# The order of 16 small products in a convolution round: down the columns of TensorE's tiles, or along the diagonals

## The chip, the core and the metric

The kernel runs on one core of a Trainium2 chip. The metric is the device time of one execution in microseconds (us); lower is better. Three runs of the kernel before took 5010.55, 5017.47 and 5027.52 us; the median is 5017.47 us. A core has five engines, each with an instruction stream of its own: TensorE (PE in the profile; its weight loads are listed apart as PEld), VectorE (DVE), ScalarE (ACT), GpSimd (POOL) and SyncE (SP, which only issues transfers here).

## What is computed

Two layers on a tensor of 4 x 512 x 64 x 64 in fp32. The first is a linear attention with a multi-scale branch; the second works on image gradients. Cut to the part that bears on the change:

```
q, k, v = h @ wq.T, h @ wk.T, h @ wv.T                       # 512 channels each
dw = conv(qkv, dw_kernel, groups=3*512)                      # 5x5, one filter per channel
pw = conv(dw, pw_kernel, groups=3*64)                        # 1x1, 8 channels to 8
f = concat(qkv, pw).reshape(B, -1, 24, N)                    # heads of 8 + 8 + 8 channels
query, key = relu(f[:, :, :8]), relu(f[:, :, 8:16]); value = f[:, :, 16:]
out = (value_pad @ key.T) @ query, divided by its last row
y = bn(conv1x1(out, proj_kernel)) + x
# second layer: Sobel, Laplace and diagonal gradients of y, four 1x1 branches with
# GELU, channel attention, a 1x1 fuse, layer norm over channels, GELU, + y
```

The change is in the pair `dw`, `pw` for keys and queries: a 5x5 convolution per channel and then a mix of 8 channels to 8. The kernel does both at once, as one 5x5 convolution from 8 channels to 8 whose weights are the products of the two.

## The kernel before

For each of the 4 images, four groups of 128 channels are worked through (class `Group`). A group first makes keys and values (`keys_and_values`), then queries (`queries`). Projections (`project`, line 268) leave a 128 x 512 strip: 128 channels, and 8 rows of the image that lie 4 apart. Line 283 copies each strip by four transfers on ScalarE's queue into the input tile of the convolution, `inps[t]`, of shape [128, 4, 17, 64]: the partition is 32 i + 4 x (channel in its eight) + (row modulo 4), the second index n picks one of four blocks of channels, the third is a block of four image rows.

`convolve` (line 394) does one half of the image for keys or queries: 2 kinds x 2 halves x 16 groups = 64 calls. It takes four PSUM banks (`quad_tiles`), one for each row group i of 32 partitions. A call has ten rounds: five horizontal offsets dx, in the order 0, -2, -1, 1, 2, and two vertical blocks b. A round has 16 products of 32 x 32 weights with 32 x 512 data (504 or 496 columns where dx cuts off the border). Product (i, j) reads rows 32 i to 32 i + 31 of the input's block j, so it uses row group i of TensorE, and writes partitions 32 j to 32 j + 31 of bank i, so it uses column group j. TensorE's array of 128 x 128 thus works as 16 tiles of 32 x 32, and in a round each tile gets one product. All ten rounds add up in the same banks.

After the call, ScalarE takes each bank through a Relu (line 415 for keys, line 421 for queries), and later `conv_turn`, `correlate`, `conv_denominators` and `conv_divide` use what it leaves. The weights `mat` are made by GpSimd (line 247); there are two buffers for them, so the next ones wait until `convolve` has finished with the old.

The order of TensorE's instructions is written out by hand: the pool context of line 107 (`manual_schedule` for TensorE) keeps it as the program issues it. `keys_and_values` and `queries` list the steps of a group with an estimate of TensorE time each, and in `run` every step is followed by so much of the later stages of the image before (projection out, line 661; edge maps and branches, line 738; fuse, line 848) as falls due by those estimates. `convolve` is one step, of estimate 10.6. Nothing else is put between its 160 products. The waits between engines are semaphores that the framework attaches to the first instruction which needs them.

Of the kernel before, what the change touches and what calls it, by code (L numbers as in the profile page):

```python
# [83 lines left out]
def _span(d, n):  # L84

    return max(0, -d), n - max(0, d)
# [3 lines left out]
def conv_seq_kernel(  # L90
    ctx: ExitStack, tc, x, wqkv, dpk, wtab, proj, projc, pwk, bn0, consts, vec, watt1, batt1, watt2, wbr, wfuse, out
):
    nc = tc.nc
# [15 lines left out]
    def work_tile(name, n=512):  # L109
        return work.tile([P, 512], F32, tag="w", name=name)[:, :n]  # L110
# [4 lines left out]
    def quad_tiles(name):  # L115
        return [psum.tile([P, 512], F32, tag="quad", name=name) for _ in range(4)]

    def squares(ap):

        return ap.rearrange("p (b x n) -> p n x b", b=4, n=4)  # L120

    def rows(ap, width=W):
        return ap.rearrange("p (r c) -> p r c", c=width)
# [21 lines left out]
    inps = {}  # L145
# [80 lines left out]
    class Group:  # L226
# [167 lines left out]
        def convolve(self, t, half):  # L394
            banks = quad_tiles("cv")
            last = len(DXS) * 2 - 1
            for n, (dx, b) in enumerate((dx, b) for dx in DXS for b in range(2)):
                c0, c1 = _span(dx, W)
                for j in range(4):
                    for i in range(4):  # L400
                        q = slice(32 * i, 32 * i + 32)
                        nc.tensor.matmul(  # L402
                            rows(banks[i])[32 * j : 32 * j + 32, :, c0:c1],
                            lhsT=self.mat[t][q, j, (dx + 2) * 8 + 4 * b : (dx + 2) * 8 + 4 * b + 4, :],
                            rhs=inps[t][q, j, 8 * half + b : 8 * half + b + 8, c0 + dx : c1 + dx],
                            start=(n == 0), stop=(n == last),
                        )
            outs = []
            for i in range(4):
                o = work_tile("co")  # L410
                if t == KEY:
                    if half == 0 and i == 0:
                        self.ksum = mini.tile([P, 4, 4], F32, name="ksum")
                    for a in range(2):
                        nc.scalar.activation(  # L415
                            o.rearrange("p (n a x b) -> p a n x b", n=4, a=2, b=4)[:, a],
                            squares(banks[i][:, 256 * a : 256 * a + 256]), AF.Relu,
                            accum_out=self.ksum[:, 2 * half + a, i : i + 1],
                        )
                else:  # L420
                    nc.scalar.activation(o, banks[i], AF.Relu)
                outs.append(o)
            self.conv[t] = outs
# [536 lines left out]
    for n, cur in enumerate(groups):  # L960
# [5 lines left out]
        if n and n % NG == 0:  # L966
            last = groups[n - 1]
# [8 lines left out]
    last = groups[-1]  # L976
# [142 lines left out]
```

## Time and profile before

| What | us |
|---|---|
| median of three runs | 5017.47 |
| the profiled execution | 5033.35 |
| its span, from the first instruction to the last | 5031.6 |
| TensorE busy with matmuls in it | 4694.3 |
| of which line 402, the products of `convolve` | 728.3 |
| VectorE busy | 2083.3 |
| ScalarE busy | 1581.8 |

The granted clock of TensorE averages 0.971 in this execution. Times in the sums below are made against the profiled execution and then set against the median. In a row of the groups, "x" is the number of records, "busy" the time in which at least one of them ran, and "mean" the length of a single one. The records of matmuls overlap, and their ends are modelled, so the mean of a matmul (593 ns at line 402) is no price; the distance between starts is. A row's last part says how long the engine was idle before its instructions and what ended that. "issue" there means that nothing the profile shows was being waited for.

### The profile page before, as it was taken

To read this page: it belongs to the slowest core of one execution; us is meant where nothing else is said; L and a number is where in the kernel's file an instruction comes from. 1 tells how busy PE (TensorE), PEld (TensorE's weight loads), DVE (VectorE), ACT (ScalarE), POOL (GpSimd) and SP (SyncE) were. 2 spreads that over 40 slices of the span, in tenths; PEclk is the share of its full clock that TensorE was granted. 3 is DMA by queue.
4 is the path that set the end of the run, shared out by engine and by line. 5 is a ranking of instruction groups with operands and counts; after the bars stand their busy time and mean duration, and the time that the engine had idled before them with its cause. 6 is when DMAs were issued, how large, how long until landed. Compare 5 with 4: busy or idle time off the path is not lost. (4 is left out here: it accounts for less than half of the span.)

```text
span 5031.6 us, 106279 instructions
## 1 busy us (share of the span) xinstructions
PE 4694.3 (93%) x46140; PEld 2689.2 (53%) x46140; DVE 2083.3 (41%) x2761; ACT 1581.8 (31%) x2712; POOL 397.3 (8%) x298
## 2 busy tenths in 40 slices
PE   9999999999999999799899999989999899899887
PEld 5655654455666554354465656445446565444333
DVE  1222222115565533311355553441125555447955
ACT  2112111003454423200245442430014445214765
POOL 0000000000000012100000000220000000000445
PEclk9999999999999999899999999999999999899998
DMA  6434467775666566677565566647665555575435
GB/s 198 138 119 134 134 192 194 162 163 161 193 190 189 180 187 189 192 177 167 152 189 189 186 192 183 207 153 217 149 173 176 171 173 170 162 166 144 165 125 163
DMA packets 627940, 864.04 MB, mean 172 GB/s; under 512 B 324073, under 2 KB 381449, under 8 KB 609041
## 3 DMA queue, kind: packets, MB, share of 16 engines
q1 hardware_dynamic: 548880, 756.51, 52.4%
q10 hardware_dynamic: 78592, 100.74, 6.3%
q8 instruction: 362, 5.93, 0.5%
q14 instruction: 106, 0.86, 0.1%
HBM read 575.93 MB, written 213.98 MB: 157 GB/s over the span
## 5 line engine op out<-in xcount | busy, mean ns | idle before, releaser
L268 PE MATMUL proj<-xt,w_sb 128*128 128x512 f32 x2048 | 955.9, 610 | 56.7 <-DMA xt<-in_x 34.6
L661 PE MATMUL yps<-hd,fold_sb 128*128 128x512 f32 x2048 | 907.8, 599 | 18.5 <-DMA hd<-heads 16.2
L402 PE MATMUL cv<-inp,mat 32*32 32x512 f32 x20480 | 728.3, 593 | 36.0 <-issue 28.2
L268 PEld LDWEIGHTS proj<-xt,w_sb 128*128 128x128 f32 x2048 | 382.7, 194 | 528.0 <-issue 451.6
L661 PEld LDWEIGHTS yps<-hd,fold_sb 128*128 128x128 f32 x2048 | 386.1, 191 | 511.0 <-issue 458.8
L402 PEld LDWEIGHTS cv<-inp,mat 32*32 32x32 f32 x20480 | 419.8, 103 | 313.1 <-issue 151.9
L848 PE MATMUL zps<-ef,wf_sb 128*128 128x512 f32 (+1 forms) x1056 | 473.4, 601 | 36.4 <-DMA ef<-ef 19.4
L290 PEld LDWEIGHTS val<-w_sb,xt 128*128 128x128 f32 x4096 | 470.6, 192 | 33.2 <-issue 25.9
L290 PE MATMUL val<-w_sb,xt 128*128 128x128 f32 x4096 | 485.2, 277 | 0.1
L738 PE MATMUL br<-maps,wbr_sb 128*128 128x256 f32 (+1 forms) x1792 | 474.2, 418 | 3.7 <-DVE s_sb L335 2.9
L274 ACT COPY strip<-proj 128x512 f32<-128x512 f32 x256 | 149.3, 583 | 932.5 <-PE proj L268 912.0
L666 DVE SCALAR_TENSOR_TENSOR yt<-yps,shift,xr 128x512 f32<-128x512 f32 x128 | 96.0, 750 | 836.5 <-PE yps L661 780.0
L738 PEld LDWEIGHTS br<-maps,wbr_sb 128*128 128x128 f32 x1792 | 340.9, 193 | 146.9 <-issue 102.0
L457 PE MATMUL corr<-near,ckt 128*32 128x160 f32 x8192 | 333.7, 315 | 40.3 <-DMA near<-near 32.9
L848 PEld LDWEIGHTS zps<-ef,wf_sb 128*128 128x128 f32 x1056 | 205.3, 198 | 285.5 <-issue 235.9
L247 POOL TENSOR_TENSOR mat<-dp_sb 128x1280 f32<-128x1280 f32 x32 | 76.7, 2398 | 3484.8 <-PE cv L402 2882.9
L457 PEld LDWEIGHTS corr<-near,ckt 128*32 128x32 f32 x8192 | 257.2, 111 | 136.1 <-issue 78.6
L714 DVE TENSOR_TENSOR maps<-dv 128x1054 f32<-128x1054 f32 (+1 forms) x112 | 158.0, 1411 | 376.3 <-PE br L738 376.2
L318 ACT ACTIVATE kt<-tr 128x512 f32<-128x512 f32 x128 | 75.9, 593 | 529.8 <-PE tr L316 401.2
L366 DVE RECIPROCAL rec<-rec 128x512 f32<-128x512 f32 x64 | 214.4, 3351 | 1.7
L746 ACT ACTIVATE ef_o<-br,shift,scale 128x256 f32<-128x256 f32 (+1 forms) x224 | 131.4, 590 | 228.1 <-PE br L738 210.4
L415 ACT ACTIVATE co<-cv 128x256 f32<-128x256 f32 x256 | 94.0, 398 | 331.1 <-PE cv L402 310.6
(127 smaller groups left out, 4049.2 us busy)
## 6 DMA issues: line engine op xcount, KB each, us to landing
xt<-in_x SPq DMA_DIRECT2D x316, 512.0 KB
near<-near SPq DMA_DIRECT2D x512, 264.0 KB
inp<-strip ACTq DMA_DIRECT2D x1024, 64.0 KB
win<-y SPq DMA_DIRECT2D x96, 396.0 KB
near<-vt SPq DMA_DIRECT2D x512, 66.0 KB
y<-yt SPq DMA_DIRECT2D x128, 264.0 KB
heads<-q SPq DMA_DIRECT2D x128, 256.0 KB
cheads<-cq SPq DMA_DIRECT2D x128, 256.0 KB
```

What stands on the lines that cost most here:

```text
L268: nc.tensor.matmul(ps, lhsT=self.w[t][:, c, :], rhs=xs[self.b, j][c], start=(c == 0), stop=(c == NCH - 1))
L274: nc.scalar.copy(s, ps)
L290: nc.tensor.matmul(ps[:, ts(c, P)], lhsT=xs[self.b, j][n][:, ts(c, P)], rhs=self.w[VALUE][:, n, :], start=(n == 0), stop=(n == NCH - 1),)
L366: nc.vector.reciprocal(rec, rec)
L402: nc.tensor.matmul(rows(banks[i])[32 * j : 32 * j + 32, :, c0:c1], lhsT=self.mat[t][q, j, (dx + 2) * 8 + 4 * b : (dx + 2) * 8 + 4 * b + 4, :],
L457: nc.tensor.matmul(self.banks[jj][32 * i : 32 * i + 32, 160 * b : 160 * b + 160], lhsT=self.held["c", i][:, at : at + 32], rhs=v[:, 4 * n ...
L661: nc.tensor.matmul(ps, lhsT=fold_sb[g // NG][:, g % NG, ts(c, P)], rhs=hd[g], start=(g == 0), stop=(g == 2 * NG - 1),)
L666: nc.vector.scalar_tensor_tensor(yt[:, :, 1 : W + 1], rows(ps), shift0[:, c : c + 1], rows(xr), ALU.add, ALU.add)
L714: nc.vector.tensor_sub(flat[:, half : 3 * half - 2], dvs[:, 2 : 2 * half], dvs[:, 0 : 2 * half - 2])
L738: nc.tensor.matmul(rows(ps), lhsT=wbr_sb[:, k, c, :], rhs=rows(maps[:, slot[k], c % 2, :], WB)[:, :, 0:W], start=(c == 0), stop=(c == NCH ...
L746: nc.scalar.activation(o[:, n, :], parts[n], AF.Gelu, bias=shift1[:, k : k + 1], scale=scale1[:, k : k + 1], accum_out=pool_sb[:, k, u : u ...
L848: nc.tensor.matmul(ps, lhsT=wf_sb[:, k, ts(c, P)], rhs=ef[k], start=(k == 0), stop=(k == 3))
```

## The change

The two loops of a round, j outside and i inside, become one loop over the 16 pairs. It runs over d from 0 to 3 outside and i inside, and takes j = (i + d) modulo 4. Before, the order is (0,0), (1,0), (2,0), (3,0), (0,1), (1,1) and so on. After, it is (0,0), (1,1), (2,2), (3,3), (0,1), (1,2), (2,3), (3,0) and so on. The products themselves, their operands and the flags for the first and last round stay the same, and nothing else in the kernel is edited.

```diff
@@ -396,15 +396,15 @@
             last = len(DXS) * 2 - 1
             for n, (dx, b) in enumerate((dx, b) for dx in DXS for b in range(2)):
                 c0, c1 = _span(dx, W)
-                for j in range(4):
-                    for i in range(4):
-                        q = slice(32 * i, 32 * i + 32)
-                        nc.tensor.matmul(
-                            rows(banks[i])[32 * j : 32 * j + 32, :, c0:c1],
-                            lhsT=self.mat[t][q, j, (dx + 2) * 8 + 4 * b : (dx + 2) * 8 + 4 * b + 4, :],
-                            rhs=inps[t][q, j, 8 * half + b : 8 * half + b + 8, c0 + dx : c1 + dx],
-                            start=(n == 0), stop=(n == last),
-                        )
+
+                for i, j in ((i, (i + d) % 4) for d in range(4) for i in range(4)):
+                    q = slice(32 * i, 32 * i + 32)
+                    nc.tensor.matmul(
+                        rows(banks[i])[32 * j : 32 * j + 32, :, c0:c1],
+                        lhsT=self.mat[t][q, j, (dx + 2) * 8 + 4 * b : (dx + 2) * 8 + 4 * b + 4, :],
+                        rhs=inps[t][q, j, 8 * half + b : 8 * half + b + 8, c0 + dx : c1 + dx],
+                        start=(n == 0), stop=(n == last),
+                    )
```

## The prediction

> **What bounds the kernel now.** I read the page first, for the engine that is always busy and the share of the changed line in it.
>
> ```profile
> span 5031.6 us, 106279 instructions
> PE 4694.3 (93%) x46140; PEld 2689.2 (53%) x46140; DVE 2083.3 (41%) x2761; ACT 1581.8 (31%) x2712; POOL 397.3 (8%) x298
> ...
> L402 PE MATMUL cv<-inp,mat 32*32 32x512 f32 x20480 | 728.3, 593 | 36.0 <-issue 28.2
> ...
> L402 PEld LDWEIGHTS cv<-inp,mat 32*32 32x32 f32 x20480 | 419.8, 103 | 313.1 <-issue 151.9
> ```
>
> TensorE is busy 93% of the span and everything else far less, so a microsecond won or lost inside a convolution is a microsecond of the kernel, nearly one for one. The changed line has 728.3 + 36.0 us. Its 20480 records are two per product of the program (64 calls x 10 rounds x 16 products = 10240): an fp32 product appears as two passes, each with its own weight load.
>
> The question is then what holds a round. I took one call that waits for nobody, the one at 191.67 us, and read the weight loads in order of time, then the sums of that window (columns: PE, then PEld, then clock, DMA share, GB/s):
>
> ```profile
> 191.67 0.23 PEld L402 LDWEIGHTS cv<-inp,mat 32*32 32x32 f32 x32 [0.17 <-issue]
> 192.13 0.10 PEld L402 LDWEIGHTS cv<-inp,mat 32*32 32x32 f32 x1 [0.22 <-issue]
> 192.56 0.55 PEld L402 LDWEIGHTS cv<-inp,mat 32*32 32x32 f32 x32 [0.32 <-issue]
> 193.42 8.02 PEld L402 LDWEIGHTS cv<-inp,mat 32*32 32x32 f32 x255 [0.31 <-issue]
> ...
> 191.67:202.35 10.68, 10.64 (x320) 6.55 (x320) 1.00 0.39 100
> ```
>
> All 32 loads of the first round go out in 0.23 us, then nothing for 0.22 us, one load, and again nothing. So the call is not short of issue speed at its start; it fills something and then waits. It takes 10.68 us, and 1.07 us per round. The passes alone, if all 16 tiles streamed all the time, need less: pass after pass on one tile is 427 ns apart at 512 columns, 420 at 504 and 413 at 496 (starts of single records), which is 2 x (2 x 427 + 4 x 420 + 4 x 413) = 8.37 us for the ten rounds. About 2 us of each call is therefore not streaming, 64 x 2 = 128 us in the kernel. This is all that any order of the products could win.
>
> Where do the 2 us go? I followed single records in that call, in ns after its first load. A product's life is: load 26, first pass 420, 4 until the second pass, 420 of that pass, and then 191 more until something is released. The release is seen like this: the load of product k starts 611 ns after the start of the second pass of product k-17 (619 at 512 columns, 604 at 496, so always the pass plus 191), for every k I followed. Between those two lie 16 products x 4 records = 64 records. So the stream behaves as a window of fixed length: 17 products per 26 + 420 + 4 + 420 + 191 = 1061 ns, 62.4 ns per product, 998 ns per round. Ten rounds give 9.98 us, and with the last drain and the uneven start the 10.68 of the row.
>
> **The change part by part.** It removes and adds no instruction: the same 160 products per call, in another order inside each round of 16. Three things move.
>
> First, the rows. Before, i runs inside, so the row groups are 0,1,2,3,0,1,2,3; after, i runs inside again, the same sequence. Each product's predecessor on its own tile stays exactly 16 back, and bank i is still finished by product 12+i of the last round, so the Relu of line 415 or 421 that waits for a bank is released at the same place. The four waits for free banks stay at products 0 to 3. Cost: 0.
>
> Second, the columns. Before, j stays for four products and then steps; after, it steps at each. The trace before contains both kinds of step: 0 to 3 inside a column group, and every fourth step, from (3, j) to (0, j+1), which already has another row and another column. If sharing a column cost something, the two kinds would differ. The following single loads, each from its own narrow stretch of the order of time, are products 65 to 68 of the call, that is (1,0), (2,0), (3,0), (0,1):
>
> ```profile
> 195.27 0.10 PEld L402 LDWEIGHTS cv<-inp,mat 32*32 32x32 f32 x1
> 195.48 0.10 PEld L402 LDWEIGHTS cv<-inp,mat 32*32 32x32 f32 x1
> 195.70 0.10 PEld L402 LDWEIGHTS cv<-inp,mat 32*32 32x32 f32 x1
> 195.91 0.10 PEld L402 LDWEIGHTS cv<-inp,mat 32*32 32x32 f32 x1
> ```
>
> In whole ns the steps are 215, 215 and 216: the last, the diagonal one, is no shorter. In the dense stretches every step is 16 to 17 ns, across the change of column too, and in the first round every one is 6 to 7. The first round's row also shows that four products in one column run together: 16 matmuls are under way within 0.12 us.
>
> ```profile
> L402 PEld LDWEIGHTS cv<-inp,mat x30: 101/101/104, 191.7 to 191.8; 32*32 32x32 f32 x30
> L402 PE MATMUL cv<-inp,mat x16: 612/612/612, 191.7 to 191.8; 32*32 32x512 f32 x16
> ```
>
> The gain from the columns is bounded by 0 and 128 us; I take the value of the nearest row, the step of 216 against 215, that is 0.
>
> Here a rule has to be weighed. The Trainium skill, "TensorE: Matmul & The Clock Gate", Part 3, The mechanism, says that a weight load overlaps matmuls in flight only where its row group differs. The trace disagrees: product 4 has the row group of product 0, whose matmul is under way from 1 ns on, and its load starts at 27 ns, not some 600 later. Taken literally the rule would make a round 4 products x 2 passes x 420 = 3.4 us, against the measured 1.07. And it speaks against any gain here, since the order of row groups is the same. The same page's Part 1, Architectural detail, gives TensorE a queue of 64 instructions; the 64 records between release and load are that number. By that rule the order inside a round is worth 0; by a rival rule in which column neighbours hold each other, up to 128 us. I go with the window.
>
> Third, the waits on transfers. The strips reach the four blocks n = j of the input tile by four transfers each (line 283). Before, blocks 1, 2, 3 are first touched by products 4, 8 and 12 of a round; after, by products 1, 2 and 3. The waits in the first two rounds (the second touches the next strip's rows) so bunch at the head, and behind a waiting load stand all later products of the call, the Relu of lines 415 and 421 that waits for their banks, and whatever follows on TensorE. In the call at 259.36 us the loads of products 4, 8, 12 start at 26, 53 and 80 ns, their natural places: the data had landed, and moving the waits costs nothing. In the first call, at 77.94 us, they start at 98 and 237 ns instead of 54 and 80; there about 0.2 us could be exposed. What can grow is the sequencer's own time:
>
> ```profile
> L402 PEldq EVENT_SEMAPHORE  x52: 51/51/51, 73.9 to 4295.1; - x52
> ...
>   issue: 180.0, 370
>   DVE weighed L475: 19.9, 30
> ```
>
> 52 separate waits of 51 ns, 2.7 us in all. The bounds: nothing, if each moved wait fits on a load or a matmul; 6 moved waits x 51 ns x 64 calls = 19.6 us if each becomes a separate instruction and none is hidden. I take as many again as there are, half of them hidden by the full window: +1.3 us. Nothing is queued differently on SP, POOL or ACT, and no transfer changes.
>
> What the change cannot touch are the stalls of instruction supply inside calls, and the waits for banks (the row for line 475 above):
>
> ```profile
> 313.71 0.24 PEld L402 LDWEIGHTS cv<-inp,mat 32*32 32x32 f32 x32 [2.17 <-issue]
> ```
>
> Summed over the 64 calls such holes without a matmul start make some 40 us, in about half of the calls; the other half have none.
>
> The sum: the profiled execution took 5033.35 us, its span 5031.6 and 1.75 around it. 5033.35 + 0 + 0 + 1.3 = 5034.7. The median of the runs, 5017.47, is 15.9 us below that execution; the same distance gives 5018.8, say **5019 us**.
>
> **The rivals.** (a) Column neighbours do hold each other, and the 191 ns are the sign of it: then a round is paced by its passes. For it speaks that 191 ns of idle tile per life is what an interference could look like; against it the equal steps above. The bound of 128 us would be reached only in the calls without supply holes; 36 of 64 have none, 36 x 2 = 72 us, and where the supply is short a faster stream only waits longer. Between 72 and 128 I take 100, so 4919 us. (b) Only the 26 ns load of a life gets hidden, because neighbouring loads go to other columns: 26/1061 of 64 x 9.98 us = 16 us, 5001 us. For it: a load's end and its pass are in line in each life. Against it: the loads of the first round, four to a column, already start 7 ns apart. (c) Slower: the bunched waits, at the head of rounds one and two of each call. The price is the 19.6 us above, 5037 us; it decides against the kernel once a call loses more than 15/64 = 0.235 us, or 4.6 separate waits of 51 ns. The trace has 0.8 per call. (d) The change does nothing that can be measured: that is the forecast.
>
> **How the numbers follow.** 0.3% is 15 us, about what a measurement of this kernel can tell from no change. Chances: no change 0.55, (a) 0.20, (b) 0.14, (c) 0.08, and 0.03 for a cost of the columns that no row shows. Nearly all of (b) lies just over the bound, so faster is 0.34, slower 0.11. The likeliest case's own range is 5004 to 5032 us, from the spread of the three runs. The range that holds 8 in 10 must take in (b) and the larger part of (a), whose end is uncertain by its bounds: 4905 to 5032.
>
> **What would show it.** If I am right, the call that waits for nobody is again 10.6 to 10.7 us with 320 loads; single straggling loads are again 215 ns apart; line 402's busy time is within a few us of 728. For (a) the undisturbed call would fall towards 8.7 us and the groups of loads would have no pauses; for (b) to about 10.4; for (c) the number of separate waits would rise from 52 to some hundreds and the first 16 loads would take over 0.4 us. The prediction is wrong if the undisturbed call changes at all.

## The result

The changed kernel takes 5021.07 us (median of 12 runs, 5008.32 to 5030.02), the kernel before 5018.81 us in the same series (12 runs, 5009.47 to 5028.59). The ratio is 1.0006 with a 95% interval of 0.9995 to 1.0018: no change that can be measured, as forecast (5019 us). The profiled execution has a span of 5011.9 us. Its page, cut to the rows that answer to those shown of before:

```profile
span 5011.9 us, 106299 instructions
PE 4686.4 (94%) x46140; PEld 2687.4 (54%) x46140; DVE 2084.2 (42%) x2761; ACT 1580.8 (32%) x2712; POOL 400.9 (8%) x298
...
L402 PE MATMUL cv<-inp,mat 32*32 32x512 f32 (+1 forms) x20480 | 729.0, 596 | 40.1 <-issue 32.8
L402 PEld LDWEIGHTS cv<-inp,mat 32*32 32x32 f32 x20480 | 419.3, 103 | 319.1 <-issue 155.8
```

Line 402 has 729.0 us where it had 728.3, and 40.1 us of idle time before it where it had 36.0. The span is 19.7 us shorter than that of the execution profiled before, but single executions of either kernel lie about that far apart, so nothing is to be read from it.

The same undisturbed call, now at 195.03 us, shows the same shape. First the weight loads in order of time, then the call's matmuls (columns: start, length, engine):

```profile
195.03 0.23 PEld L402 LDWEIGHTS cv<-inp,mat 32*32 32x32 f32 x32 [0.17 <-issue]
195.49 0.10 PEld L402 LDWEIGHTS cv<-inp,mat 32*32 32x32 f32 x1 [0.23 <-issue]
195.91 0.55 PEld L402 LDWEIGHTS cv<-inp,mat 32*32 32x32 f32 x32 [0.32 <-issue]
196.77 8.02 PEld L402 LDWEIGHTS cv<-inp,mat 32*32 32x32 f32 x255 [0.30 <-issue]
...
195.03 10.65 PE L402 MATMUL cv<-inp,mat 32*32 32x512 f32 x320
```

The bursts and pauses are those of before, to 0.01 us. Before, the matmuls of this call took 10.64 us. From the first matmul start to the last, undisturbed calls take 10.076 us against 10.070. Products 65 to 68 are now (1,1), (2,2), (3,3) and (0,1), so every step between them has another row and another column:

```profile
198.62 0.10 PEld L402 LDWEIGHTS cv<-inp,mat 32*32 32x32 f32 x1
198.84 0.10 PEld L402 LDWEIGHTS cv<-inp,mat 32*32 32x32 f32 x1
199.06 0.10 PEld L402 LDWEIGHTS cv<-inp,mat 32*32 32x32 f32 x1
199.27 0.10 PEld L402 LDWEIGHTS cv<-inp,mat 32*32 32x32 f32 x1
```

In whole ns the steps are 217, 214 and 216, against 215, 215 and 216 before. The only thing that changed visibly is the number of separate waits, which rises from 52 to 72:

```profile
L402 PEldq EVENT_SEMAPHORE  x72: 51/51/51, 75.8 to 4289.9; - x72
```

### The profile page after: what moved, and what is told of

Same layout as the page of the kernel before. It is cut to its first block, busy times and chain, and to the rows that moved or that the text cites. A ratio compares the mean times of both kernels' runs of the same rounds, so it can differ in the third digit from the quotient of the medians.

```text
span 5011.9 us, 106299 instructions
## 1 busy us (share of the span) xinstructions
PE 4686.4 (94%) x46140; PEld 2687.4 (54%) x46140; DVE 2084.2 (42%) x2761; ACT 1580.8 (32%) x2712; POOL 400.9 (8%) x298
## 5 line engine op out<-in xcount | busy, mean ns | idle before, releaser
L402 PE MATMUL cv<-inp,mat 32*32 32x512 f32 (+1 forms) x20480 | 729.0, 596 | 40.1 <-issue 32.8
L848 PE MATMUL zps<-ef,wf_sb 128*128 128x512 f32 (+1 forms) x1056 | 472.0, 600 | 36.2 <-DMA ef<-ef 19.7
```

The costliest lines, as they stand in the source:

```text
L402: nc.tensor.matmul(rows(banks[i])[32 * j : 32 * j + 32, :, c0:c1], lhsT=self.mat[t][q, j, (dx + 2) * 8 + 4 * b : (dx + 2) * 8 + 4 * b + 4, :],
L848: nc.tensor.matmul(ps, lhsT=wf_sb[:, k, ts(c, P)], rhs=ef[k], start=(k == 0), stop=(k == 3))
```

## The experiments

The forecast rested on one claim: that a call is held by a limit on all products in flight together, 17 of them, each for 26 + pass + 4 + pass + 191 ns. If that limit belongs to each tile, row group or column group instead, the order is equally harmless here, and the reason given would still be wrong. All edits below are made to the kernel before. The kernels were run in three series, and each has its own median for the kernel before: 5003.63 us for the column, the row, the pairs and the first kernel in which the row group stays; 5005.17 us for the one product left out, the first round alone and the head in the old order; 5008.03 us for the repetition at the end. Calls are compared by the length of their matmuls where nothing disturbs them, since this repeats to 0.01 us, and the kernel by its ratio. Sums over the 64 calls come from one profiled execution of each kernel; the one of the kernel before took 5033.35 us, longer than its medians, so a few us in such a sum mean nothing.

### A column group left out, and a row group left out

```diff
                 for j in range(4):
                     for i in range(4):
+                        if j == 3 and 0 < n < last:
+                            continue
                         q = slice(32 * i, 32 * i + 32)
```

> The eight middle rounds of each call leave out the four products of column group 3, so the sums of those channels are incomplete; 12 products per round remain. Window theory (17 products in flight in all, whatever tile they use, each for two passes + 221 ns): a round is then held by its tiles alone, 2 x 420 + 4 = 844 ns instead of 998, the undisturbed call falls from 10.68 to about 9.35 us, and the kernel by 50 to 85 us to 4935 to 4970 us (calls short of instruction supply gain less). Column theory (each column group has a limit of its own, 4.25 products) and tile theory (a tile's next load waits until its last product has drained): columns 0 to 2 are as full as before, the call stays 10.68 us and the kernel near 5019 us. Row theory (a limit for each row group): as the window.

The second kernel has `i == 3` in that place.

> The eight middle rounds leave out the four products of row group 3 (incomplete sums in bank 3); 12 products per round. Window theory: as with a column left out, the undisturbed call about 9.35 us, the kernel 4935 to 4970 us. Column theory: columns now have three products a round, so the call falls too. Row theory and tile theory: row groups 0 to 2 are as full as before, the call stays 10.68 us and the kernel near 5019 us.

Measured: 4940.97 us without the column, ratio 0.9874 (0.9859 to 0.9888), and 4931.64 us without the row, ratio 0.9855 (0.9841 to 0.9870), a little under the range that was expected. An undisturbed call without the column, and one without the row, each in order of time:

```profile
2408.92 9.32 PE L404 MATMUL cv<-inp,mat 32*32 32x512 f32 x256
```

```profile
433.16 9.32 PE L404 MATMUL cv<-inp,mat 32*32 32x512 f32 x256
```

Both fall from 10.64 to 9.32 us, by the same amount. If the limit belonged to a column group, the first kernel would have kept its 10.64 us, because columns 0 to 2 were as full as ever. If it belonged to a row group, the second would have. If it belonged to a tile, both would have. So the limit is shared by all of them, and with 12 products in a round the tiles' own passes take over, as expected (9.35 us).

Over all 64 calls the time from the first matmul start to the last fell by 107.1 and 102.9 us in the profiled executions, but the kernel gained only 62.7 and 72.0 us. Where the rest went was not taken apart.

### One product of sixteen left out

```diff
                 for j in range(4):
                     for i in range(4):
+                        if (i, j) == (3, 3) and 0 < n < last:
+                            continue
                         q = slice(32 * i, 32 * i + 32)
```

> The eight middle rounds leave out one product of sixteen, that of tile (3, 3) (its 32 channels get incomplete sums). Window theory, by the recurrence with a load released by product k-17: the last matmul of an undisturbed call starts 9.76 us after its first, against 10.07 with all; with a window of 16 products it would be 10.09, with 18 it would be 9.13. The kernel gains 10 to 20 us, a ratio of 0.996 to 0.998. Any limit for each tile, row or column alone: 10.07 us and no gain, since all other tiles are as full as before.

Measured: 4978.58 us, ratio 0.9951 (0.9938 to 0.9965). The last matmul starts 9.752 to 9.756 us after the first in undisturbed calls, where 9.76 was expected for 17 products, 10.09 for 16 and 9.13 for 18. The first call of this kernel:

```profile
78.07 10.32 PE L404 MATMUL cv<-inp,mat 32*32 32x512 f32 x304
```

Fifteen tiles are as full as before and yet the call is 0.32 us shorter, which settles the size of the limit as well as its kind. The kernel gained 26.6 us by its medians and 24.5 by the ratio, more than 64 x 0.32 = 20 and than the 10 to 20 us expected. Summed over the calls of the two profiled executions, the time between first and last matmul start fell by 23.6 us, so nearly all of it lies in the calls: the disturbed ones gained more than the undisturbed.

### Two products in a row on each tile

This is the order that the limit should punish: 17 products in flight then cover only some nine tiles. "Recurrence" in what follows means the limit worked through product by product: load k waits for the release of product k-17, and the passes of one tile go one after another.

```diff
-            for n, (dx, b) in enumerate((dx, b) for dx in DXS for b in range(2)):
+            for m, dx in enumerate(DXS):
                 c0, c1 = _span(dx, W)
-                for j in range(4):
-                    for i in range(4):
+                for j, i, b in ((j, i, b) for j in range(4) for i in range(4) for b in range(2)):
+                    n = 2 * m + b
```

> All products, but the two vertical blocks b of one tile follow each other, so that each tile gets two products in a row and 17 products in flight cover only some nine tiles. Window theory: by the recurrence of the prediction (load at the release of product k-17, passes in line on one tile) a call takes about 17.3 us instead of 10.68, the kernel 6.6 x 64 = 424 us more, near 5440 us. Theories with a queue for each tile, row or column alone: every tile has the same passes to stream as before, the call changes by some 0.3 us, the kernel by less than 20 us.

Measured: 5331.24 us, ratio 1.0653 (1.0637 to 1.0669). The loads of an undisturbed call in order of time, and its matmuls:

```profile
608.66 0.23 PEld L402 LDWEIGHTS cv<-inp,mat 32*32 32x32 f32 x17 [0.17 <-issue]
609.12 0.72 PEld L402 LDWEIGHTS cv<-inp,mat 32*32 32x32 f32 x18 [0.23 <-issue]
610.16 0.10 PEld L402 LDWEIGHTS cv<-inp,mat 32*32 32x32 f32 x1 [0.33 <-issue]
...
608.66 17.32 PE L402 MATMUL cv<-inp,mat 32*32 32x512 f32 x320
```

The call takes 17.32 us, as the recurrence said (17.3). Only 17 loads go out at once where there were 32. That is near the 18 that nine tiles with two loads each would give, and fits with half of the products in flight sitting behind another on their own tile, where they cannot load yet. Every tile has the same passes to stream as before, so a queue for each tile alone would have cost some 0.3 us. The run also speaks against a shared limit on the rate, such as one on issue or on moving data: the same products would pass it in the same time in either order, and the call takes 1.6 times as long. This is the case in which the order of products matters a lot.

The kernel's loss was over-estimated: 327.6 us and not 424. Over the 64 calls of the profiled executions the time from first to last matmul start rose by 374.6 us (724.8 to 1099.4), not by 64 x 6.68 = 428. The calls that were disturbed before had time in hand. Their holes without a matmul start (those over 700 ns, less one pass, waits at the head of a call among them) shrank from 39.5 to 2.2 us. Outside the calls some waits became shorter too, such as that of line 268 for `xt`, from 34.6 to 20.3 us. What makes up the remainder was not taken apart.

### The row group stays, the column steps

```diff
-                for j in range(4):
-                    for i in range(4):
+                for i in range(4):
+                    for j in range(4):
```

> All products, with j inside and i outside: the row group stays for four products and the column group steps at each. Window theory with parallel loads: nothing changes, 10.68 us a call, 5019 us. If the loads of one row group go in line at 26 ns each, eight of them for four products take some 210 ns, 854 ns a round, still under 998: at most 0.2 us a call, 14 us in the kernel. Theory that a weight load overlaps running matmuls only of another row group: the four products of a row would go one after the other, a call of some 34 us or more and a kernel over 6000 us.

Measured: 4996.05 us, ratio 0.9987 (0.9979 to 0.9996). The undisturbed call:

```profile
192.53 10.64 PE L402 MATMUL cv<-inp,mat 32*32 32x512 f32 x320
```

The call does not change, and in its first round the loads of four products of one row group start 7 ns apart, as those of four row groups do. All four stand within 23 ns (192.525 to 192.548 us):

```profile
L402 PEld LDWEIGHTS cv<-inp,mat x4: 101/101/101, 192.5 to 192.5; 32*32 32x32 f32 x4
```

So neither reading with a role for the row group holds: the loads do not even go in line. This is the runs' answer to the rule weighed in the prediction (the Trainium skill, "TensorE: Matmul & The Clock Gate", Part 3, The mechanism), that a load overlaps running matmuls only of another row group. For these 32 x 32 fp32 tiles it does not hold as it stands. The same section also lets a load go ahead into a background weight buffer; the records do not show which buffer a load fills, so whether that is the way round the rule here stays open.

The 0.13% was not expected. In this order the waits for free banks stand at products 0, 4, 8 and 12 instead of 0, 1, 2 and 3, which could hide them. Two more runs asked for it. The first keeps the row group in the first round only:

```diff
-                for j in range(4):
-                    for i in range(4):
+                for x in range(4):
+                    for y in range(4):
+                        i, j = (x, y) if n == 0 else (y, x)
```

> Only the first round of each call keeps a row group for four products (i outside); the other nine rounds as before. If the 0.13% of the run with that order in all rounds came from the waits for free banks, which then stand at products 0, 4, 8, 12 instead of 0, 1, 2, 3: the calls that wait for banks take 10.07 instead of 10.8 us, some 17 calls x 0.7 = 12 us at most, the same ratio of 0.998 to 0.9995. If it came from the order of later rounds or was chance: ratio 1.000.

Measured: 5001.34 us, ratio 0.9994 (0.9984 to 1.0005). The second repeats the kernel with the row group staying in all rounds.

> The kernel with j inside and i outside in all rounds once more, to see whether its 0.13% is real. If the bank waits at products 0, 4, 8, 12 hide behind the products between them in all calls, or the head is otherwise better filled: a ratio of 0.998 to 0.9995 again. If it was chance: 1.000.

Measured: 5000.40 us, ratio 0.9994 (0.9986 to 1.0002). The two intervals of that kernel overlap between 0.9986 and 0.9996, and the second holds 1. A gain of some 0.1% is therefore possible and not certain from the kernel's time.

The traces place it. In six traces (the kernel before and after, the two with the row group staying, the one in the first round only, and the old head of the next experiment) the same 17 of the 64 calls wait for banks. From first to last matmul start, and without the holes further inside, these 17 take 200.7 us before and 192.5 and 192.3 us in the two profiled executions with the row group staying. The other 47 take 491.5, 489.9 and 489.8 us. Here are the first loads of one such call, before and then with the row group staying:

```profile
4227.65 0.14 PEld L402 LDWEIGHTS cv<-inp,mat 32*32 32x32 f32 x4 [0.30 <-issue]
4228.02 0.13 PEld L402 LDWEIGHTS cv<-inp,mat 32*32 32x32 f32 x2 [0.23 <-DVE weighed L475]
4228.42 1.64 PEld L402 LDWEIGHTS cv<-inp,mat 32*32 32x32 f32 x65 [0.27 <-DVE weighed L475]
```

```profile
4199.32 0.18 PEld L402 LDWEIGHTS cv<-inp,mat 32*32 32x32 f32 x16 [0.30 <-issue]
4199.69 0.15 PEld L402 LDWEIGHTS cv<-inp,mat 32*32 32x32 f32 x8 [0.19 <-DVE weighed L475]
4200.09 1.91 PEld L402 LDWEIGHTS cv<-inp,mat 32*32 32x32 f32 x66 [0.25 <-DVE weighed L475]
```

While the third bank is awaited 16 loads are out instead of 4, and for the fourth 24 instead of 6. The waits last equally long, 0.77 us from the first load to the last wait's end, but the call takes 10.64 us instead of 11.36. So this order does hide waits for banks. The 17 calls gain 8 us by it against the kernel before, and 6 us against the kernel of the next experiment, which takes 198.8 us for them with the old head. With the first round alone in this order they take 199.6 us: most of the effect needs the later rounds as well, and why was not taken apart. No kernel here is shown to beat both.

### The head of a call in the old order

```diff
-                for j in range(4):
+                for x in range(4):
                     for i in range(4):
+                        j = x if n < 2 else (i + x) % 4
```

> The diagonal order only from the third round on; the first two rounds, which wait for transfers, stay in the old order. If the 20 additional semaphore waits and the later first call come from the diagonal order at the head alone: 52 waits again instead of 72, the first call's last matmul again 10.14 us after its first instead of 10.98, and the undisturbed call unchanged, 10.07 to 10.08. In time this is at most 3 us: same as before within 0.2%. If the columns matter in later rounds, the undisturbed call changes.

Measured: 5008.79 us, ratio 1.0005 (0.9996 to 1.0014), and an undisturbed call of 10.07 us to its last matmul start. The waits:

```profile
L403 PEldq EVENT_SEMAPHORE  x52: 51/51/51, 75.7 to 4276.4; - x52
```

They are 52 again, so the additional 20 do come from the first two rounds in diagonal order. Half of what was expected with it rested on a misreading: that the changed kernel's first call, 10.98 us to its last matmul start against 10.14, was held by those waits. Its matmuls show the place where it lost the time:

```profile
79.91 8.68 PE L402 MATMUL cv<-inp,mat 32*32 32x512 f32 x260
89.21 2.25 PE L402 MATMUL cv<-inp,mat 32*32 32x496 f32 x60 [0.62 <-issue]
```

The first 260 run without a break; the gap ends 9 us into the call, long after the waits, and is one of the holes in which nothing is being waited for (the last section has their places). In the run with the old head this call has no such gap (10.16 us), but such holes fall in other calls there.

## Why the prediction was right

**What holds a round.** Right, and the part that the runs tested hardest. The limit of 17 products for all tiles together was read from starts in one call; it then gave the calls with 15, with 12 and with paired products to 0.03 us or better, before they were run.

**Rows.** Right: the cost was put at 0 because the sequence of row groups is the same. The run with the row group staying shows more, that the sequence of row groups does not matter to an undisturbed call at all.

**Columns.** Right in the value, on evidence that carried less than was put on it. The old order's diagonal step of 216 ns was set against 215 for the others. But by the prediction's own limit a load starts when product k-17 is released, so the distance between such loads is handed down from 17 products earlier; a cost of the step's own neighbours need not show there. What shows the columns to be free is the undisturbed call after the change, 10.65 us, and the 10.64 us of the order in which the column steps each time and the row group stays. Rival (a), up to 128 us, and rival (b), 16 us, fell with it. The prediction called itself wrong if that call changed at all; it changed by 6 ns to its last matmul start, 0.4 us in 64 calls, and not at all with the old order in the first two rounds (10.071 us).

**Waits on transfers.** Right in kind, and the estimate was high. The prediction took 52 more separate waits, half of them hidden, +1.3 us. There are 20 more, so 20 x 51 ns = 1.0 us at most if nothing hides them. The calls of the profiled execution, holes left out, sum to 686.0 us against 685.3. The 0.2 us expected in the first call did not show: there the first 32 loads went out within 0.23 us. Rival (c) would have needed 4.6 more separate waits per call; 20 in 64 calls are 0.3.

**Supply holes.** The prediction held that the change cannot touch them. Its 40 us in about half of the calls took in pauses at the heads of calls: 6.9 us of the 39.5 before, 6.8 of the 44.0 after. All but 0.7 us of these are waits for banks; the 0.7 us are the long first passes of one call that starts at a granted clock of 0.50. The rest, further inside the calls, is 28 holes of 32.6 us in 23 calls before and 28 holes of 37.2 us in 27 calls after. Which of the possible places open differs from execution to execution, so the difference is not put down to the change.

**One for one.** The premise that a microsecond in a convolution is nearly one of the kernel was not needed for a forecast of no change. The runs with larger effects show it to be loose: 0.6 to 0.7 with 12 products in a round, 0.9 with pairs (327.6 us of 374.6).

**The sum.** 5019 us against a measured 5021.07, with an interval of the ratio that holds 1. The 1.3 us put down for waits cannot be told from 0 at this spread, so the closeness to 2 us is luck; "no change" is what was shown. Rival (a) was counted from 5019 us, (b) and (c) from 5017, which decides nothing.

## What to carry to other kernels

Before an order is changed to avoid a conflict, look in the trace for places where the old order already takes the wanted step, and compare those steps with the others: here every fourth step was diagonal and no faster. Ask first what sets the distance between such steps; where a release 17 products back sets it, only a run of the other order decides. In a stream of small products on TensorE, count what is in flight: here 17 fp32 products at a time over a life of two passes and 221 ns set the rate. Of the orders tried, only the one that makes products queue on their own tile changed it (+6.5% of the kernel with two in a row), and what helped was fewer products. When an experiment takes work away from one row, column or tile only, it tells a shared limit from a private one.

## What the runs showed of the hardware that was not expected

The size of the limit agrees with the queue of 64 instructions that the Trainium skill gives TensorE ("TensorE: Matmul & The Clock Gate", Part 1, Architectural detail), at four records per fp32 product; that it counts records and not products was not tried, since no kernel here has another number of records per product.

TensorE does not seem to start these matmuls in the order of the program. Before, product 4's first pass starts 27 ns after the call's first matmul and product 0's second pass 453 ns after it. A record does not name its product; the reading rests on 16 starts within 100 ns, one for each tile, and 16 more a pass later.

The holes inside calls, up to 2.3 us long before and 3.0 after, with no releaser in the profile, have fixed places. One call before has two of them:

```profile
305.20 7.24 PE L402 MATMUL cv<-inp,mat 32*32 32x512 f32 x188
313.71 4.38 PE L402 MATMUL cv<-inp,mat 32*32 32x504 f32 x128 [1.27 <-issue]
319.64 1.02 PE L402 MATMUL cv<-inp,mat 32*32 32x496 f32 x4 [1.54 <-issue]
```

They are 128 matmuls apart, which with their loads is 256 records. The page before lists the transfers that bring instructions (packets, MB, share of the DMA engines' time):

```profile
q8 instruction: 362, 5.93, 0.5%
```

That is 16 KB for each packet, and 64 bytes for each of TensorE's 92852 records, so 256 records for each packet. Counted from the start of the kernel, all 28 holes inside calls before, and all 28 after, stand after 193 records and a whole multiple of 256. In each the last such packet had landed 1.1 to 1.7 us before the stream went on. So the name that the prediction gave them, supply of instructions, fits in place and in time; no run changed the supply itself.

They follow the rate of the stream. Inside the calls they make 32.6 us before, 16.0 and 18.3 us with a quarter of the products left out of eight rounds, and nothing in the slow paired order, which has as many matmuls and loads as before (its 2.2 us lie at the heads of two calls). At the rate of an undisturbed call 256 records last 4.0 us, in the paired order 6.7 us. Where two holes follow each other in one call before, their ends lie 4.6 to 6.5 us apart, between the two.
